# Two transformer layers on one core: the second layer's steps joined to the first's

## The chip, the cores and the metric

One core of one Trainium2 chip runs the whole kernel. Its engines work side by side, each in its own order: TensorE (PE in the profile) for matmuls, with its weight loads (PEld); VectorE (DVE); ScalarE (ACT), which alone computes exponentials and the like; GpSimd (POOL), which can't read the matmul banks; and SyncE (SP), which issues most DMAs. Matmuls write into eight banks of 128 x 512 floats. The metric is the device time of one execution in microseconds, as the median of several runs.

## The reference

The input is `x` of 8 batches x 512 tokens x 256 features, in float32. Two layers follow. Each normalizes `x` by layernorm to `xn` and adds an attention and a feed-forward branch of the same `xn`:

```
x = x + attn0(xn) + experts(xn)          # layer 0
x = x + attn1(xn) + ffn1(xn)             # layer 1, xn of the new x
attn0:   16 heads of 16, softmax(q k^T) v
experts: each token goes to one of 8 experts (argmax), layernorm, 256 -> 1024 relu -> 256, gated
attn1:   causal attention with q, k, v -> ctx; convolution over 3 tokens of ctx -> q2;
         causal attention with q2 and the same k, v; output projection
ffn1:    x U1 (rank 64) V1 + b1 -> gelu (tanh form) -> U2 (rank 64) V2 + b2
```

## The kernel before

**Jobs and steps.** Attention is cut into jobs of four heads of one batch: 32 in layer 0, 64 in layer 1 (32 with q, "firsts", and 32 with q2, "seconds", which come seven jobs later). A job of layer 0 has 8 steps and one of layer 1 has 6 (`STEPS`). In one step `run` issues matmuls for the row maxima of one job (`scores`, L345, reduced on DVE at L362 or L365) and, interleaved with them on other 32-row strips of the array, the scores for the exponentials of the job 12 steps behind (`exps`, L394, exponentials on ACT at L421, in layer 1 with a small mask matmul, L412). Between the two a job's maxima are transposed and DMAed into spare rows of q (`shift`, L375 to L382). `attend` (L434) multiplies by the values at the places that `AV_AT` gives.

**The order of the rest.** All five engines run in the order in which the code issues (`manual_schedule`). Other work is cut into pieces in a `Work` list, each with an earliest step, a deadline and a cost; `fill` issues some at the end of each step, ahead of that step's `attend`. In layer 0 a `stream` is paced beside it at `MOE_PER_STEP` of cost a step: first norms, routing, then 23 expert blocks (L772 features, L794 hidden, L815 output) and then the second norms (`SECOND`), one entry a step: gathers of the experts' rows by POOL (`g`), their weighted sum into `acc` on DVE (`+` and `P`, L522), statistics on DVE (`s`, `S`), the closing of a group with a square root on ACT (`c`, L247), normalizing on ACT (`n`, `N`, L257) and transposes to features (`f`, L266).

**The seam.** Layer 0's `run` comes to its end before anything else starts. Then comes a stage for the FFN alone: per batch one `ffn_in` (L965), four pairs of `ffn_hidden` (L977, gelu by ACT at L983) and `ffn_rank` (L990, summed up in bank 7), and `ffn_out` (L1002, L1006), with the second norms of batches 4 to 7 (`THIRD`) between. Only then does `run` start on layer 1 with a list of its own, `todo1`. Its pieces are q and k projections (`l1_project`, L293, 512 columns), values (L303), convolution (`convolve`, L1072, in halves of 256 columns, taken up on DVE), `to_tokens` (L1090), `to_features` (L266) and `project_out` (L1124).

**Banks in layer 1.** `banks_alone` gives three banks to the maxima, three to the scores, one to AV and one, bank 7, to all pieces.

Of the kernel before, what the change touches and what calls it, by code (L numbers as in the profile page):

```python
# [9 lines left out]
F32 = mybir.dt.float32  # L10
# [10 lines left out]
NB = 8  # L21
# [17 lines left out]
LEAD = (12, 12)  # L39
EARLY = 4  # L40
MOE_PER_STEP = 2.08
LAG = 7

# [17 lines left out]

SECOND = (
    "g0 g1", "", "", "+0", "P0 g2", "+1", "P1 g3", "", "+2", "P2 g4", "+3", "P3 g5", "s0", "S0 s1", "S1 s2", "S2 s3",
    "S3", "c", "n0", "N0 n1", "f0 N1", "n2 f1", "N2", "n3 f2", "N3", "f3",
)

THIRD = (
    "+4", "P4 s4 g6", "S4 +5", "P5 s5 g7", "S5 +6", "P6 s6", "S6 +7", "P7 s7", "S7", "c", "n4", "N4 f4", "", "n5",
    "N5 f5", "", "n6", "N6 f6", "", "n7", "N7 f7",
)  # L70

# [14 lines left out]
    {2: (0,), 4: (1,), 6: (2,), 8: (3,)}, {5: (0,), 6: (1, 3), 7: (2,)}, {2: (0,), 4: (1, 3), 6: (2,)},  # L86
# [10 lines left out]
class Work:  # L97
# [20 lines left out]
    def fill(self, t, per_step, most):  # L118
# [3 lines left out]
        while True:  # L122
# [19 lines left out]
            n += 1  # L142
# [10 lines left out]
def block_kernel(ctx: ExitStack, tc: tile.TileContext, x, a0_wqk, a0_bqk, a0_wv, a0_bv, cent, experts,  # L153
# [40 lines left out]
    for _ in range(2):  # L194
        value_buffer(const)
    banks = [psum.tile([P, S], F32, name=f"bank{i}") for i in range(8)]
# [14 lines left out]
    def banks_alone():  # L211
        share_banks(mx=banks[:3], sc=banks[3:6], av=banks[6:7], mm=banks[7:])

# [75 lines left out]
    def project(w, col, src, nm):  # L289

        ps = bank()
        for k in range(2):
            nc.tensor.matmul(  # L293
                ps, lhsT=w[:, k, col : col + P], rhs=src[:, k, :], start=(k == 0), stop=(k == 1)
            )
        return ps

    def values(w, bias, src, dst, h, nm):
        ps = bank()
        for j in range(2):  # L300
            c = 2 * h + j
            for k in range(2):
                nc.tensor.matmul(  # L303
                    ps[:, j * D : (j + 1) * D],
                    lhsT=src[:, k, c * P : (c + 1) * P],
                    rhs=w[:, k, :],
                    start=(k == 0),
                    stop=(k == 1),
                )
        for j in range(2):  # L310
            nc.vector.tensor_tensor(
                dst[:, 2 * h + j, :, 0:HD],
# [6 lines left out]
    class Job:  # L319


        def __init__(self, nm, causal, scale, v, g, done, pool):
            self.nm, self.causal, self.scale, self.v, self.g, self.done = nm, causal, scale, v, g, done
            self.pool = pool
# [7 lines left out]
        def scores(self, i):  # L332
# [24 lines left out]
            def after():  # L357
                for h in (2 * pr, 2 * pr + 1):
                    for qc, at, nk in parts:
                        src = heads[h % 2][:, at : at + nk]  # L360
                        if not self.causal:
                            nc.vector.tensor_reduce(self.m[:, qc, h, :], src, AX.X, ALU.max, negate=True)  # L362
                            continue
                        junk = l1.tile([P, S], BF16, tag="junk", name=f"jk{self.nm}_{qc}_{h}", bufs=1)
                        nc.vector.tensor_tensor_reduce(  # L365
                            out=junk[:, :nk], in0=src, in1=cmask[:, S - nk :], scale=1.0, scalar=-3e38,
# [17 lines left out]
        def exps(self, i):  # L384
# [22 lines left out]
            def after():  # L407
                if self.causal:
# [7 lines left out]
                e = self.pool.tile(  # L416
                    [P, 2, n], F32, tag=f"e{blocks[0]}" if self.causal else "e", name=f"e{self.nm}_{i}",
                    bufs=3 if self.causal else 4,
                )
# [22 lines left out]
    def run(jobs, work_of, layer, per_step, most):  # L442
        steps, lead = STEPS[layer], LEAD[layer]
        end = steps * len(jobs)
        if layer == 1:
            for job in jobs[-(lead // steps) :]:
                job.seq = 2
        attends = {}
        for j, job in enumerate(jobs):
            av_at = AV_AT[job.seq]  # L450
            for i, blocks in av_at.items():
                attends.setdefault(lead + steps * j + i, []).append((job, blocks, i == max(av_at)))

        def attend(t):
            for job, blocks, last in attends.pop(t, ()):
                for kc in blocks:
                    job.attend(kc, kc == 0, last and kc == blocks[-1])
                if last:
                    job.done(job, t)

        work_of.first()
        for t in range(max(attends) + 1):
            work_of.t = t
            if layer == 0 and t == lead:
                banks_alone()
            mm, after = [], []
            if t >= lead or layer == 1:
                maxima = (t,)
            else:

                maxima = (t, t + 1) if t % 2 == 0 else ()

            scores = (t - lead,) if t < end else (t - lead, t - lead + 1) if (t - end) % 2 == 0 else ()
            if t == end:
                banks_last()
            for at, call in [(i, Job.scores) for i in maxima] + [(i, Job.exps) for i in scores]:
                j, i = divmod(at, steps)
                if 0 <= j < len(jobs):
                    m, a = call(jobs[j], i)
                    mm.append(m)  # L480
                    after.append(a)
# [6 lines left out]
            work_of.fill(t, per_step, most)  # L488
            attend(t)
        work_of.drain()  # L490

    fgs, yns, norms_of = {}, {}, {}

    def second(pieces):

        for p in pieces.split():
            do, b = p[0], int(p[1:] or 0)
            if do == "c":
                norms_of[max(norms_of)].close()
                continue  # L500
            if do == "s":
                first = b < EARLY
                bs = range(EARLY) if first else range(EARLY, NB)
                if bs[0] not in norms_of:
                    norms_of[bs[0]] = Norms(mid, bs, "dc"[first], False)
            n = norms_of.get(0 if b < EARLY else EARLY)
            if do == "g":

                fgs[b] = mid.tile([P, NC, D], F32, tag="fg", name=f"fg{b}", bufs=2)
                for c in range(NC):  # L510
                    t = b * NC + c
                    nc.gpsimd.indirect_dma_start(
                        out=fgs[b][:, c, :],
# [4 lines left out]
            elif do in "+P":  # L518
                for c in range(2) if do == "+" else range(2, NC):
                    t = b * NC + c  # L520
                    a = acc[b][:, c, :]
                    nc.vector.scalar_tensor_tensor(  # L522
                        a, fgs[b][:, c, :], alpha[:, t : t + 1], a, ALU.mult, ALU.add
                    )
            elif do in "sS":
                n.stats(n.bs.index(b), range(2) if do == "s" else range(2, NC))
            elif do in "nN":
                if do == "n":
                    yns[b] = work.tile([P, NC, D], F32, tag="o", name=f"yn{b}")
                n.norm(n.bs.index(b), yns[b], range(2) if do == "n" else range(2, NC))  # L530
            else:
                t = big.tile([P, 2, S], F32, tag="xT", name=f"yT{b}")
                for k in range(2):
                    to_features(yns[b], t, 0, k, f"c{b}")
                xT1.append(t)
# [9 lines left out]
    mids = ExitStack()  # L545
    mid = mids.enter_context(tc.tile_pool(name="mid", bufs=1, side="right"))

    u1_sb = mid.tile([P, 2, 2, RANK], F32, name="u1_sb")
    v1_sb = mid.tile([P, FF], F32, name="v1_sb")
    v2_sb = mid.tile([P, D], F32, name="v2_sb")  # L550
    fb1_sb = mid.tile([P, NFC], F32, name="fb1_sb")
    u2_sb = mid.tile([P, NFC, RANK], F32, name="u2_sb")
    ob_sb = const.tile([P, D], F32, name="ob_sb")

    def load_ffn():
        for i in range(2):
            r = slice(i * RANK, (i + 1) * RANK)
            nc.sync.dma_start(out=u1_sb[:, :, i, :], in_=u1)
            nc.sync.dma_start(out=v1_sb[r, :], in_=v1)
            nc.sync.dma_start(out=v2_sb[r, :], in_=v2)  # L560
        nc.sync.dma_start(out=fb1_sb, in_=f_b1)
# [706 lines left out]
```

## Time and profile before

| | us |
|---|---|
| three runs | 2121.31, 2112.47, 2118.51 |
| median | 2118.51 |
| the profiled execution, its own time | 2120.86 |
| the profiled execution, first to last instruction | 2118.7 |

| stretch (us) | what runs |
|---|---|
| 0 to 951 | layer 0 with norms, routing and experts; the last expert output ends near 949 |
| 951 to 1020 | the rest of layer 0's attention, second norms of batches 0 to 3 |
| 1020 to 1133 | the FFN stage, second norms of batches 4 to 7 |
| 1133 to 1186 | layer 1's first 17 steps, without AV |
| 1186 to 2119 | layer 1 |

The profile's lines show one execution. "L345" is line 345 of the kernel before. A float32 matmul shows as two instructions (passes), a transpose as one. Their ends are modelled, so the distance from start to start tells more than the duration. The granted clock is the share of TensorE's full speed that the throttle allowed.

### The profile page before, as it was taken

How to read it: one execution, taken by the hardware profiler on the slowest of the kernel's cores; microseconds unless marked ns; L12 is line 12 of the kernel's file. 1: busy time of each engine (PE TensorE's matmuls, PEld its weight loads, DVE VectorE, ACT ScalarE, POOL GpSimd, SP SyncE). 2: the span in 40 equal slices, each digit the busy share in tenths (PEclk: the TensorE clock that was granted, in tenths of full speed). 3: DMA queues.
4: the chain of work that ended last, by engine and by line, in shares of the span. 5: the costliest groups of instructions: out<-in, count | busy, mean ns of one | idle time of the engine just before them, and what ended most of it. 6: DMA issues, size and time to landing. Idle time of an engine off the chain costs nothing.

```text
span 2118.7 us, 35530 instructions
## 1 busy us (share of the span) xinstructions
PE 2010.6 (95%) x13672; PEld 1016.4 (48%) x13672; DVE 1228.6 (58%) x3565; ACT 867.8 (41%) x1690; POOL 175.6 (8%) x222
## 2 busy tenths in 40 slices
PE   5797999999999999998898999999999999999998
PEld 3333555555555555552233445455555545554554
DVE  5564455555555555557424676666766666666763
ACT  4342333333333333335551444444444444444434
POOL 4153000000000000004211000000000000000000
PEclk8698999999999999999999899999999999999999
DMA  6014212212121221202100000000000000000000
GB/s 211 13 45 143 104 54 105 101 58 105 53 105 53 105 105 53 105 11 78 40 1 1 2 2 2 2 2 12 2 12 2 12 2 12 2 11 2 2 12 21
DMA packets 37192, 93.53 MB, mean 44 GB/s; under 512 B 5920, under 2 KB 28064, under 8 KB 34080
## 3 DMA queue, kind: packets, MB, share of 16 engines
q0 software_dynamic: 6384, 59.78, 7.7%
q1 hardware_dynamic: 29792, 30.56, 4.5%
q8 instruction: 107, 1.75, 0.3%
q10 hardware_dynamic: 848, 0.93, 0.1%
q14 instruction: 61, 0.50, 0.1%
HBM read 70.03 MB, written 20.45 MB: 43 GB/s over the span
## 4 chain that ended last, share of the span: by engine, by line
PE 83%; DVE 6%; issue 5%; DMA 4%; ACT 2%; POOL 1%; ACTq 0%; POOLq 0%; DVEq 0%; SPq 0%
PE bank L345 27%; PE bank L434 12%; PE bank L794 8%; PE bank L815 8%; PE bank L293 5%; PE bank L1072 4%; PE bank L412 4%; DMA hs_d<-h,pos_i 4%; PE bank L394 3%; PE bank L303 2%; PE bank L1090 2%; PE bank L1124 1%; DVE m L362 1%; PE bank L977 1%; PE bank L990 1%
## 5 line engine op out<-in xcount | busy, mean ns | idle before, releaser
L421 ACT ACTIVATE e<-bank 128x512 f32<-128x512 f32 (+1 forms) x1280 | 638.9, 552 | 921.4 <-PE bank L394 462.8
L345 PE MATMUL bank<-k,q 32*128 32x512 f32 (+3 forms) x3072 | 765.1, 538 | 24.6 <-DVE m L362 20.3
L394 PE MATMUL bank<-q,k 32*128 32x512 f32 (+3 forms) x3072 | 682.6, 535 | 2.4 <-DVE m L362 1.6
L365 DVE CUSTOM_DVE_ANT_0 jk<-bank,cmask 128x512 bf16<-128x512 f32 (+3 forms) x1024 | 502.8, 491 | 241.7 <-PE bank L345 162.4
L345 PEld LDWEIGHTS bank<-k,q 32*128 32x128 f32 x3072 | 301.4, 187 | 388.4 <-issue 165.2
L362 DVE TENSOR_REDUCE m<-bank 128x1 f32<-128x512 f32 x512 | 328.8, 685 | 152.5 <-PE bank L394 122.7
L434 PE MATMUL bank<-e,v 128*32 128x512 f32 (+3 forms) x3072 | 317.8, 501 | 0.7 <-ACT e L421 0.7
L394 PEld LDWEIGHTS bank<-q,k 32*128 32x128 f32 x3072 | 266.0, 186 | 12.2 <-issue 6.1
L794 PE MATMUL bank<-hsT,w 128*128 128x256 f32 x736 | 181.2, 392 | 6.4 <-DVE hsT L777 6.4
L794 PEld LDWEIGHTS bank<-hsT,w 128*128 128x128 f32 x736 | 135.1, 192 | 74.5 <-issue 58.9
L815 PE MATMUL bank<-w,hT 128*128 128x256 f32 x736 | 170.7, 385 | 0.0
L815 PEld LDWEIGHTS bank<-w,hT 128*128 128x128 f32 x736 | 137.5, 192 | 36.6 <-issue 18.7
L434 PEld LDWEIGHTS bank<-e,v 128*32 128x32 f32 x3072 | 67.7, 108 | 139.7 <-issue 133.0
L412 PE MATMUL bank<-mask_t,ident_bf 128*128 128x128 bf16 (+1 forms) x768 | 123.4, 244 | 0.0
L412 PEld LDWEIGHTS <-ident_bf 128*128 128x128 bf16 x768 | 43.9, 97 | 155.7 <-issue 140.6
L807 DVE TENSOR_SCALAR hT<-bank,w 128x256 f32<-128x256 f32 x92 | 44.5, 484 | 113.7 <-ACT hT L805 113.7
L1072 PE MATMUL bank<-ctxT,cw_sb 128*128 128x256 f32 x384 | 90.0, 383 | 2.1 <-DVE q L283 1.8
L365 DVE DVE_READ_ACCUMULATOR2_ANT m<- 128x1 f32 x1024 | 85.0, 83 | 0.0
L805 ACT ACTIVATE hT<-bank,w 128x256 f32<-128x256 f32 x92 | 43.7, 475 | 92.9 <-PE bank L794 92.9
L824 DVE TENSOR_TENSOR f<-bank,w 128x256 f32<-128x256 f32 x46 | 19.5, 425 | 105.4 <-PE bank L815 105.4
L285 ACT ACTIVATE k<-bank,bqk,rows 128x512 f32<-128x512 f32 x64 | 46.3, 774 | 81.7 <-PE bank L293 72.4
L1072 PEld LDWEIGHTS bank<-ctxT,cw_sb 128*128 128x128 f32 x384 | 70.1, 189 | 13.2 <-DVE q L283 3.2
(186 smaller groups left out, 1383.5 us busy)
## 6 DMA issues: line engine op xcount, KB each, us to landing
q<-mT SPq DMA_DIRECT2D x384, 2.0 KB
hs_d<-zeros SPq DMA_DIRECT2D x23, 256.0 KB
hs<-hs_d SPq DMA_DIRECT2D x23, 256.0 KB
fs_d<-f SPq DMA_DIRECT2D x23, 256.0 KB
acc<-in_x SPq DMA_DIRECT2D x8, 512.0 KB
out<-acc SPq DMA_DIRECT2D x8, 512.0 KB
cw_sb<-in_conv_w SPq DMA_DIRECT2D x1, 768.0 KB
wqk<-in_a_wqk ACTq DMA_DIRECT2D x1, 512.0 KB
```

The lines of the kernel that those rows point to most:

```text
L285: nc.scalar.activation(dst, ps, AF.Identity, bias=bias[:, half : half + 1], scale=rows[:, half : half + 1])
L293: nc.tensor.matmul(ps, lhsT=w[:, k, col : col + P], rhs=src[:, k, :], start=(k == 0), stop=(k == 1))
L345: lambda h=h, qc=qc, at=at, nk=nk: nc.tensor.matmul(heads[h % 2][:, at : at + nk], lhsT=self.q[h * PH : (h + 1) * PH, qc * P : (qc + 1) * ...
L362: nc.vector.tensor_reduce(self.m[:, qc, h, :], src, AX.X, ALU.max, negate=True)
L365: nc.vector.tensor_tensor_reduce(out=junk[:, :nk], in0=src, in1=cmask[:, S - nk :], scale=1.0, scalar=-3e38, op0=ALU.add, op1=ALU.max, acc ...
L394: lambda h=h, kc=kc, at=at, lo=lo: nc.tensor.matmul(heads[h % 2][:, at : at + S - lo], lhsT=self.k[h * PH : (h + 1) * PH, kc * P : (kc + 1 ...
L412: nc.tensor.matmul(heads[h][:, : len(blocks) * P], lhsT=ident_bf, rhs=mask_t[:, : len(blocks) * P], start=False, stop=True,)
L421: nc.scalar.activation(e[:, h, :], heads[h][:, :n], AF.Exp, scale=self.scale)
L434: nc.tensor.matmul(self.av[h * PH : (h + 1) * PH, lo:], lhsT=self.v[:, kc, 4 * self.g + h, :], rhs=es[h // 2][:, h % 2, :], start=first, s ...
L794: nc.tensor.matmul(ps[:, i * TB : (i + 1) * TB], lhsT=w[:, O_W1 + k * FF + fc * P : O_W1 + k * FF + (fc + 1) * P], rhs=self.hsT[:, k, :], ...
L815: nc.tensor.matmul(ps[:, 0:D], lhsT=self.hT[:, fc, j * P : (j + 1) * P], rhs=w[:, O_W2 + fc * D : O_W2 + (fc + 1) * D], start=(fc == 0), s ...
L1072: nc.tensor.matmul(ps[:, :w], lhsT=cw_sb[:, k, tap, c * P : (c + 1) * P], rhs=ctxT[b % 2][:, k, tap + lo : tap + lo + w], start=(k == 0 an ...
```

## The change

- **One run.** `run` takes the jobs of both layers. Layer 1's first job has its step 0 at step 256 (`T0`), right after layer 0's last maxima, so its maxima run beside layer 0's last 12 steps of exponentials. The separate FFN stage is gone. All pieces are in one list, `todo`.
- **Opening layer 1.** When the expert stream ends (step 240 in the order of instructions), the gathers of batch 0 are issued, layer 1's buffers are made and cleared, and all its weights are loaded by SP (`open_layer1`). `SECOND`, `THIRD` and three further entries for each of batches 5 to 7 are put at fixed steps; norms are closed in four groups instead of two.
- **Sums on GpSimd.** The gathered rows' weighted sum is two GpSimd instructions a chunk instead of one on DVE. There is one gather buffer instead of two.
- **FFN units.** A unit (`ffn_unit`) is two hidden chunks at place 3 of a job; the place of a step t is `(t - TS) % 6`, with `TS` = 268, layer 1's first step of exponentials. The gelu is made of Identity and Square on ACT, an add and a product on GpSimd, Tanh on ACT and a product on DVE, in the steps after; `rank` comes five steps later and sums on DVE.
- **Halved pieces in four of six steps.** `fill_evenly` spreads the pieces' costs over places 1 to 4 of a job; places 5 and 0 have AV. Projections have 256 columns (64 pieces for 32), the convolution 128 (64 for 32), values and output projection one chunk of tokens. In places 1 to 4 the pieces have bank 6 as well as bank 7 (`banks_between`).
- **AV in two bursts:** kc 0 at place 5, then 1, 3 and 2 at place 0 of the next.
- The convolution's results are taken up by ACT instead of DVE. The causal mask is bf16. Tiles are used in turn from fixed rings (`take_turn`) where pools gave them out.

The core of the diff:

```diff
-MOE_PER_STEP = 2.08
+MOE_PER_STEP = 2.07
+NORM_GROUPS = ((0,), (1,), (2, 3), (4, 5, 6, 7))
 SECOND = (
-    "g0 g1", "", "", "+0", "P0 g2", "+1", "P1 g3", "", "+2", "P2 g4", "+3", "P3 g5", "s0", "S0 s1", "S1 s2", "S2 s3",
-    "S3", "c", "n0", "N0 n1", "f0 N1", "n2 f1", "N2", "n3 f2", "N3", "f3",
+    "g0", "+0", "", "s0", "S0", "c0 n0", "N0", "f0", "g1", "+1", "", "", "s1", "", "S1", "c1 n1", "N1", "f1", "g2", "+2",
+    "", "", "s2", "", "S2", "g3", "+3", "", "", "s3", "", "S3", "c2 n2", "N2", "f2",
 )
 AV_AT = (
-    {2: (0,), 4: (1,), 6: (2,), 8: (3,)}, {5: (0,), 6: (1, 3), 7: (2,)}, {2: (0,), 4: (1, 3), 6: (2,)},
+    {2: (0,), 4: (1,), 6: (2,), 8: (3,)}, {5: (0,), 6: (1, 3, 2)}, {2: (0,), 4: (1, 3), 6: (2,)},
 )
...
+    def banks_between(free):
+        share_banks(mm=banks[6:] if free else banks[7:])
...
+        def free(t):
+            return t < TS or 0 < (t - TS) % STEPS[1] < 5
...
+            if t >= end:
+                todo.fill(t, 99.0, 1)
+            elif "pool" in l1:
+                if t >= TS + STEPS[1]:
+                    banks_between(free(t))
+                todo.fill_evenly(t, free)
+            else:
+                todo.fill(t, MOE_PER_STEP, 99)
...
-                    nc.vector.scalar_tensor_tensor(
-                        a, fgs[b][:, c, :], alpha[:, t : t + 1], a, ALU.mult, ALU.add
-                    )
+                    nc.gpsimd.tensor_scalar(fg[:, c, :], fg[:, c, :], alpha[:, t : t + 1], None, ALU.mult)
+                    nc.gpsimd.tensor_tensor(a, a, fg[:, c, :], ALU.add)
...
+            later.close()
+            l0.close()
+            second(SECOND[0])
+            open_layer1()
+            t = todo.t
+            at = [(t + i, p) for i, p in enumerate(SECOND)][1:]
+            at += [(t + len(SECOND) + THIRD_EVERY * i, p) for i, p in enumerate(THIRD)]
+            at += [(jobs1_at(b) - LATE + 2 * i, f"{p}{b}") for b in range(5, NB) for i, p in enumerate("nNf")]
...
+    def ffn_unit(b, c2):
+        hid, cub = wide(7), wide(3)
+        ps = [bank() for _ in range(2)]
+        for i in range(2):
+            fc, r = 2 * c2 + i, slice(i * RANK, (i + 1) * RANK)
+            nc.tensor.matmul(
+                ps[i], lhsT=l1["v1"][r, fc * P : (fc + 1) * P], rhs=l1["pT"][r, :], start=True, stop=True
+            )
+        for i in range(2):
+            fc = 2 * c2 + i
+            nc.scalar.activation(
+                hid[:, i * S : (i + 1) * S], ps[i], AF.Identity, bias=l1["fb1"][:, fc : fc + 1]
+            )
+        nc.scalar.activation(cub, hid, AF.Square, scale=GELU_C ** 0.5)
+        def times(i):
+            nc.vector.scalar_tensor_tensor(c, c, 1.0, u, ALU.add, ALU.mult)
+        def cube(i):
+            nc.gpsimd.tensor_scalar(c, c, 1.0, None, ALU.add)
+            nc.gpsimd.tensor_tensor(c, c, u, ALU.mult)
+        def tanh(i):
+            nc.scalar.activation(c, c, AF.Tanh, scale=GELU_A)
...
+        for after, f, i in ((1, cube, 0), (1, cube, 1), (2, tanh, 0), (3, tanh, 1), (3, times, 0), (4, times, 1)):
+            todo.add(t + after, t + after, 0.0, lambda f=f, i=i: f(i))
+        todo.add(t + 5, t + 5, 0.9, rank)
...
-    def convolve(n, half):
+    def convolve(n, quarter):
...
-            take(ps[:, :w], i, cb_sb[:, c, :], job.q[:, lo : lo + w], "v")
+            take(ps, i, l1["cb"][:, c, :], job.q[:, lo : lo + P], "s")
...
+    def ffn_at(n):
+        return TS + STEPS[1] * (1 + n * 17 // 10) + 3
```

## The prediction

> **What bounds the kernel now.** I read the page's busy line first, then the stages in stretches of 50 us, then TensorE's order of time in one job of layer 1 and across the seam between the layers.
>
> ```profile
> PE 2010.6 (95%) x13672; PEld 1016.4 (48%) x13672; DVE 1228.6 (58%) x3565; ACT 867.8 (41%) x1690; POOL 175.6 (8%) x222
> ```
> ```profile
> 900.00:950.00 50.00, 50.00 (x275) 27.33 (x273) 26.58 (x49) 16.97 (x32) 1.46 (x2) 1.00 0.02 6
> 950.00:1000.00 50.00, 45.07 (x241) 14.02 (x234) 37.71 (x92) 26.66 (x48) 25.89 (x26) 0.93 0.30 88
> ...
> 1050.00:1100.00 50.00, 45.52 (x177) 17.31 (x176) 13.39 (x25) 29.15 (x49) 9.42 (x4) 1.00 0.00 1
> ...
> 1150.00:1200.00 50.00, 48.14 (x234) 22.04 (x232) 28.11 (x107) 13.70 (x26) 0.00 (x0) 0.69 0.01 1
> ...
> 1500.00:1550.00 50.00, 49.60 (x430) 27.56 (x429) 34.01 (x123) 22.29 (x46) 0.00 (x0) 1.00 0.02 8
> ```
> The columns are PE, weight loads, DVE, ACT, POOL (us and count), then granted clock. Layer 0 with the experts (900) and layer 1 (1500) are full of TensorE work. The poor stretch is the seam. At 950 the experts have ended, DVE (37.7 of 50) paces the last scores. The FFN stage runs TensorE alone with DVE idle. At 1150 layer 1 starts with half-filled steps at a clock of 0.69.
>
> ```profile
> 984.66 0.59 PE L345 MATMUL bank<-k,q 32*128 32x512 f32 x1
> ...
> 1028.30 1.13 PE L977 MATMUL bank<-pT,v_sb 64*128 64x512 f32 x4
> 1029.36 1.08 PE L990 MATMUL bank<-gT,u_sb 128*64 128x512 f32 x4
> 1030.36 1.13 PE L977 MATMUL bank<-pT,v_sb 64*128 64x512 f32 x4
> ...
> 1185.63 1.94 PE L434 MATMUL bank<-e,v 128*32 128x512 f32 x8
> ...
> 1506.65 0.28 PE L345 MATMUL bank<-k,q 32*128 32x128 f32 x2
> ...
> 1506.76 0.28 PE L345 MATMUL bank<-k,q 32*128 32x128 f32 x2
> ...
> 1506.98 0.39 PE L412 MATMUL bank<-mask_t,ident_bf 128*128 128x256 bf16 x2
> 1507.30 1.20 PE L345 MATMUL bank<-k,q 32*128 32x256 f32 x3
> ```
> Starts matter here, since ends are modelled. Layer 0's last score is at 984.7, layer 1's first AV at 1185.6. A gelu unit costs TensorE 1.06 + 1.00 us. So **the FFN stage (1020 to 1133) is itself nearly all TensorE work**; moving it into layer 1 does not hide it. What can be won is the seam's emptiness.
>
> **The change, by three stretches.** The sum is made on the profiled execution: span 2118.7, its own time 2120.9, the median of three 2118.5; a difference is carried over as it is.
>
> *To 951 us (last expert output):* same pieces. The expert stream ends one step later (step 240, not 239, by the order of instructions) with the same work before it. Rings of tiles for pools, the bf16 mask, and the FFN loads moved: zero, as TensorE covers them.
>
> *The seam, 951 to the first AV of layer 1, today 234 us,* becomes steps 241 to 272. Sixteen steps still carry layer 0's scores; such steps took 949.3 to 984.7 today, 2.2 us each: 36. Eleven steps pair layer 1's maxima with layer 0's exponentials: 1.07 for four 512-wide tiles, 0.5 for AV, about 0.9 for a piece: 27. Five more are plain layer 1: 11. That is 74. On top come waits. POOL issues the first gathers until about 957.5 (4 x 1.25 from 952.8), clears the new buffers (the 1.81 memset row and smaller ones, 3), then does the first sums, four times 0.553 + 0.726: 966. The statistics are put on DVE three steps after the gather, about 958, and everything behind them on DVE, the maxima above all, waits: 5 to 8. SP also issues 2.95 MB of loads in that step (by their shapes; 0.36 to 0.43 each to issue, 6 us); the next query-row DMAs behind them come eight steps later and are safe, but the gathers share the engines: 0 to 8. Each closing of norms puts two table loads (1.283 each) on ACT with exponentials queued behind: about 3, three times. The statistics of the three further batches may wait likewise, 0 to 5 each. I take 6 + 2 + 9 + 2 = 19; from both sides 6 to 41. **Seam 93, so 141 saved** (119 to 154).
>
> *Layer 1, 1185.6 to the end, today 933 us.* Prices are TensorE start to start.
>
> ```profile
> L1072 PE MATMUL bank<-ctxT,cw_sb 128*128 128x256 f32 x384 | 90.0, 383 | 2.1 <-DVE q L283 1.8
> L1072 PEld LDWEIGHTS bank<-ctxT,cw_sb 128*128 128x128 f32 x384 | 70.1, 189 | 13.2 <-DVE q L283 3.2 <-ACT ctxT L270 1.3
> L983 ACT ACTIVATE gT<-bank,fb_sb 128x512 f32<-128x512 f32 x64 | 40.4, 684 | 49.0 <-PE bank L977 49.0
> L899 POOL TENSOR_TENSOR acc<-acc,og 128x256 f32<-128x256 f32 x32 | 23.2, 726 | 603.7 <-DVE og L895 603.6
> L1148 POOL TENSOR_TENSOR acc<-acc,ob_sb 128x1024 f32<-128x1024 f32 x8 | 18.8, 2351 | 74.7 <-DVE acc L1006 74.7
> ```
> - FFN arrives: 32 x (1.06 + 1.00), seven entry projections at 1.92, eight outputs at 1.92: **+95**. Features of batches 2 to 7, 48 transposes at 0.147: **+7**.
> - Halved projections: a pass of 256 columns streams in 0.213 and a burst adds about 0.15. 54 halves at 1.0 against 28 wholes at 1.87: +2. Values and output projection cut likewise: +3.
> - Convolution in quarters: 64 pieces of 12 passes of 128 columns replace 32 of 12 passes of 256, which took 3.0 each, 96 in all. The weight loads double. A load's record lasts 0.189, more than the 0.107 that 128 columns need, so the price lies between 64 x (12 x 0.107 + 0.15) = 92 and 64 x (12 x 0.189 + 0.15) = 155. The lines at 1506.65 and 1506.76 are nearest: two passes of 128 columns, each with its own 128-column load of 0.19, start 0.11 apart, so loads overlap. But those are 32-row tiles. I take 0.12: 102, **+6** (-4 to +59).
> - AV in two bursts: 1.00 + 1.00 + 0.57 holds about 0.15 a burst beyond streaming; 64 fewer: **-10**.
> - The wait at 1507.30 (the second head starts 0.7 late, DVE still reducing) comes once in most jobs. Longer, filled steps cover it: **-25** (0 to -42).
> - New waits. A unit puts two Identity (0.68 each by the gelu row) and a Square (about 1.0) on ACT; the next exponentials queue behind these 2.4 us, and with three score banks a short next step waits. Each cube half on POOL is 2 x 0.553 + half of 2.35 = 2.3. Counted from the start of the unit's step, its matmuls end at +2.3, ACT's three at +4.8, the cubes at +7.2 and +9.5; with steps of 2.5, 2.9, 1.8 and 2.7 us the tanhs reach the head of ACT at +6.8 and +9.5. The fit is tight: each microsecond that POOL is late blocks ACT, the exponentials and the AV copy behind it. In steps 278 and 314 the cubes stand behind a batch's sums (5.1 on POOL). The last closing adds 3. **+30** (0 to +64).
>
> Other engines keep room. DVE (34 of 50) gains about 47 for the products, 22 for the rank sums, 41 for features, statistics and outputs, and loses 32 as ACT takes over the convolution: some 70% of the new stretch. ACT gains about 165 (56%).
>
> Sum: 95 + 7 + 5 + 6 - 10 - 25 + 30 = +108, so 1041. **Total 951 + 93 + 1041 = 2085 span, 33 less; 2085 on the median too.**
>
> **Two rules of the Trainium skill.** "TensorE: Matmul & The Clock Gate", Back-to-back issue gap, speaks against quarters: pairs of load and matmul sustain about 81 ns at 128 columns where streaming alone takes 56. Scaled so, a pass would be 0.155 and the sum 27 higher, about 2112; the trace's 0.11 on row tiles disagrees. "ScalarE: Activation LUTs", Table sets, puts exp and tanh in one set, sqrt in another, at about 2.7 us a load; the trace's loads last 1.283, and by the page's figure four closings would cost some 11 more.
>
> **The rivals.**
> 1. *Slower: quarters are bound by weight loads.* For it: 0.189 is longer than 0.107. Against: the overlapped row-tile loads. At 0.189 the convolution costs 53 more than I took: 2138. It turns the result slower than 2129 from about 0.177 a pass.
> 2. *No change: the cube chain blocks ACT.* For it: the fit to a few tenths; ACT is in order and exponentials are the feed of AV. One extra microsecond in each of 32 units: 2117. Against: units stand 6 or 12 steps apart.
> 3. *The seam does not close.* If the chain gather, sums, statistics, norm, features, projection is late for both first batches, TensorE drains and the clock falls as at 1150: 40 more, 2125. Against: 15 steps lie between the gather and the first layer 1 score.
> 4. *More is won:* all hidden DVE waits go (17 more) and the new waits stay at 10 (20 less): 2048.
>
> **How the numbers follow.** A measurement here tells about 0.5% from no change, so faster is below 2108, slower above 2129. Forecast 0.50 (2060 to 2108), rival 4 0.12, rivals 2 and 3 0.21 (mostly 2108 to 2129, a third of it beyond), rival 1 or several together 0.17. Faster 0.62, same 0.14, slower 0.24. The convolution (+53), the waits (+34) and the seam (+22) do not all fall at once; the range 2040 to 2145 leaves about 0.18 outside.
>
> **What would show it.** Right: no stretch without layer-1 or layer-0 scores, first layer-1 AV near 1044, no low clock after 951, jobs of about 16.5 us where they take 14.5 now, convolution passes starting 0.11 to 0.13 apart. Wrong: passes near 0.19; ACT idle before tanh with POOL as releaser and TensorE waiting for exponentials; DVE idle before the first statistics by more than 8 us; a cold clock near 960.

## The result, and the profile after

The changed kernel takes 2146.7 us (median of four runs, 2142.2 to 2150.6) where the kernel before took 2117.8 beside it: the ratio is 1.0138, with a 95% interval of 1.0106 to 1.0170. It is slower by 29 us; the prediction was 33 us faster. The profiled execution has a span of 2147.5.

The page's busy line and the same 50 us stretches (PE, weight loads, DVE, ACT, POOL, granted clock, DMA):

```profile
PE 1984.3 (92%) x14168; PEld 1027.1 (48%) x14168; DVE 1252.2 (58%) x3611; ACT 995.2 (46%) x1950; POOL 403.1 (19%) x414
```
```profile
900.00:950.00 50.00, 49.24 (x268) 26.07 (x266) 25.44 (x47) 16.25 (x30) 1.45 (x2) 1.00 0.02 6
950.00:1000.00 50.00, 42.12 (x208) 14.13 (x204) 27.56 (x58) 23.04 (x42) 27.54 (x35) 0.86 0.34 88
1000.00:1050.00 50.00, 44.96 (x233) 18.97 (x233) 30.03 (x111) 23.63 (x44) 24.63 (x27) 0.90 0.08 22
1050.00:1100.00 50.00, 44.53 (x316) 21.65 (x315) 32.09 (x118) 27.71 (x53) 20.71 (x19) 0.90 0.05 12
...
1500.00:1550.00 50.00, 46.23 (x404) 24.46 (x404) 32.85 (x118) 26.19 (x54) 7.84 (x5) 1.00 0.04 12
```

TensorE's busy time fell by 26 us, yet the span grew by 29. In the middle of layer 1 (1500) TensorE now stands at 46.2 of 50, where it was 49.6; no other engine is near full. Something makes TensorE wait. The view of TensorE's waits over layer 1 (line, what it waited for, total us, times, longest) names it; first the kernel before, then the seven longest of the changed kernel's 39 rows:

```profile
PE bank L1090 <- DVE q L283: 4.0, 14, 0.3
PE bank L1090 <- ACT avs L1106: 2.6, 2, 2.0
PE bank L1072 <- DVE q L283: 1.8, 8, 0.2
PE bank L266 <- DVE o L1094: 0.4, 1, 0.4
```
```profile
PE bank L1124 <- DVE mT L429: 11.2, 12, 1.7
PE bank L356 <- DVE mT L429: 7.0, 6, 1.3
PE bank L426 <- ACT avs L1158: 7.0, 12, 1.9
PE bank L1142 <- DVE mT L429: 4.3, 8, 0.9
PE bank L320 <- ACT xT L1052: 3.9, 5, 0.8
PE bank L1142 <- ACT avs L1158: 3.5, 3, 1.9
PE bank L1174 <- DVE mT L429: 3.2, 3, 1.3
```

The first list is all there was: 9 us. The seven rows of the second hold 40 of 75 us. There, quarters of the convolution (L1124), values (L356), AV transposes (L1142) and output projections (L1174) wait for `mT`: the copy out of the bank that `shift` had filled (31 us in all rows). One such wait in the changed kernel's timeline, on TensorE, DVE and ACT (start, length, [idle before, and who ended it]):

```profile
1352.46 0.58 ACT L1158 COPY avs<-bank 128x512 f32<-128x512 f32 x1
...
1353.60 0.27 PE L426 MATMUL bank<-ident,m 128*16 128x128 f32 x1
...
1353.71 0.60 PE L1142 MATMUL bank<-ident,avs 128*128 128x128 f32 x4
1353.79 0.56 DVE L416 CUSTOM_DVE_ANT_0 junk<-bank,cmask 128x384 bf16<-128x384 f32 x1
...
1355.19 0.56 DVE L416 CUSTOM_DVE_ANT_0 junk<-bank,cmask 128x384 bf16<-128x384 f32 x1
...
1355.67 0.27 DVE L429 TENSOR_SCALAR mT<-bank 16x128 f32<-16x128 f32 x1
1356.00 1.60 PE L1124 MATMUL bank<-ctxT,cw 128*128 128x128 f32 x12 [1.69 <-DVE mT L429]
```

In a job's second step `shift`'s small transpose takes one of the two piece banks (in 12 of the 64 jobs it waits for ACT's copy of AV, as that bank held AV), and the AV transposes take the other. The third piece wants the first bank again. Its copy needs 0.27 us, but it stands on DVE behind the maxima of the whole step and ends two microseconds after the transpose. The kernel before packed one piece a step, so nobody stood behind.

I summed TensorE's order by starts, from the first AV of layer 1 to TensorE's last instruction, and took out the idle time that the trace marks. The work is 915 us before (from 1185.6) and 1004 after (from 1060.3); the marked waits are 8.8 before and **75.3** after. This count of work and waits is used below. A stall that the trace does not mark counts as work in it.

### The profile page after: what moved, and what is told of

Its sections match the earlier page's. It is cut to its first block, busy times and chain, and to the rows that moved or that the text cites. A ratio compares the mean times of both kernels' runs of the same rounds, so it can differ in the third digit from the quotient of the medians.

```text
span 2147.5 us, 36982 instructions
## 1 busy us (share of the span) xinstructions
PE 1984.3 (92%) x14168; PEld 1027.1 (48%) x14168; DVE 1252.2 (58%) x3611; ACT 995.2 (46%) x1950; POOL 403.1 (19%) x414
## 5 line engine op out<-in xcount | busy, mean ns | idle before, releaser
L469 ACT ACTIVATE e<-bank 128x512 f32<-128x512 f32 (+1 forms) x1280 | 639.4, 552 | 830.6 <-PE bank L445 480.5
L397 PE MATMUL bank<-k,q 32*128 32x512 f32 (+1 forms) x3056 | 724.5, 536 | 25.5 <-DVE m L414 23.6
L416 DVE CUSTOM_DVE_ANT_0 junk<-bank,cmask 128x512 bf16<-128x512 f32 (+3 forms) x1024 | 502.5, 491 | 352.3 <-PE bank L397 277.2
L397 PEld LDWEIGHTS bank<-k,q 32*128 32x128 f32 x3056 | 267.7, 186 | 410.2 <-issue 160.1
L445 PEld LDWEIGHTS bank<-q,k 32*128 32x128 f32 x3072 | 250.0, 185 | 16.5 <-ACT e L469 9.6
L1065 POOL TENSOR_SCALAR xT<-xT 128x512 f32<-128x512 f32 x64 | 95.3, 1489 | 605.5 <-ACT xT L1057 524.7
L347 PE MATMUL bank<-xT,wqk 128*128 128x256 f32 (+1 forms) x384 | 134.2, 479 | 11.9 <-DVE q L337 4.8
L938 POOL TENSOR_TENSOR acc<-acc,og 128x256 f32<-128x256 f32 x32 | 23.2, 725 | 591.2 <-DVE og L934 591.1
L463 PE MATMUL bank<-mask_t,ident_bf 128*128 128x128 bf16 (+1 forms) x768 | 122.9, 243 | 0.0
L463 PEld LDWEIGHTS <-ident_bf 128*128 128x128 bf16 x768 | 43.9, 97 | 155.0 <-issue 139.7
L1124 PE MATMUL bank<-ctxT,cw 128*128 128x128 f32 x768 | 100.4, 281 | 13.1 <-DVE mT L429 11.2
L1124 PEld LDWEIGHTS bank<-ctxT,cw 128*128 128x128 f32 x768 | 92.0, 194 | 23.3 <-DVE mT L429 14.3
L347 PEld LDWEIGHTS bank<-xT,wqk 128*128 128x128 f32 x384 | 68.8, 196 | 70.1 <-issue 42.2
```

The costliest lines, as they stand in the source:

```text
L347: nc.tensor.matmul(ps, lhsT=w[:, k, col : col + P], rhs=src[:, k, tokens], start=(k == 0), stop=(k == 1))
L397: lambda h=h, qc=qc, at=at, nk=nk: nc.tensor.matmul(heads[h % 2][:, at : at + nk], lhsT=self.q[h * PH : (h + 1) * PH, qc * P : (qc + 1) * ...
L416: nc.vector.tensor_tensor_reduce(out=l1["junk"][:, :nk], in0=src, in1=l1["cmask"][:, S - nk :], scale=1.0, scalar=-3e38, op0=ALU.add, op1= ...
L445: lambda h=h, kc=kc, at=at, lo=lo: nc.tensor.matmul(heads[h % 2][:, at : at + S - lo], lhsT=self.k[h * PH : (h + 1) * PH, kc * P : (kc + 1 ...
L463: nc.tensor.matmul(heads[h][:, : len(blocks) * P], lhsT=ident_bf, rhs=mask_t[:, : len(blocks) * P], start=False, stop=True,)
L469: nc.scalar.activation(e[:, h, :], heads[h][:, :n], AF.Exp, scale=self.scale)
```

## The experiments

All were measured beside the kernel before, on one chip per group. The kernel before took 2120 to 2125 in these groups and 2118 beside the changed kernel, so where two runs of different groups are compared, a range is given: by the medians, by the ratios and by the spans of the profiled executions.

**The order of the two banks.** After, each step starts the ring afresh, so `shift` always takes the bank that AV has just held.

```
     def banks_between(free):
-        share_banks(mm=banks[6:] if free else banks[7:])
+        if len(rings["mm"]) != 1 + free:
+            share_banks(mm=[banks[7], banks[6]] if free else banks[7:])
```

> The changed kernel with one edit: the ring of the two piece banks is no longer reset in every step, and begins with bank 7 at place 1. As it stands, the first piece of each step always takes bank 6: at place 1 that is the shift, which must wait until ACT has copied AV out of it (TensorE waited 7.0 us for that in all), and a step's first piece meets the one before it in the same bank. Theory (banks): that 7.0 and some of the 10 us of waits for q, k and Identity go, 8 to 18 us less than the changed kernel's 2147, so about 2134; the waits behind the shift's copy on DVE stay near 30. Rival (the tanh chain or the convolution's quarters are what costs): no more than 3 us less.

Measured: 2139.4 us, ratio 1.0079 (1.0055 to 1.0103). `shift`'s wait for ACT's copy (7.0 us) is gone, and now the AV transposes wait 6.6 for it; the waits for `mT` stay at 29. Some 7 to 12 us of the loss are the order.

**Shift ahead of the maxima.** On top of the bank order, `shift` is issued ahead of that step's maxima on DVE, not behind them.

```
+            if t in shift_at:
+                banks_between(free(t))
+                shift_at.pop(t)()
             for f in after:
                 f()
...
-        todo.add(t0 + STEPS[1], t0 + STEPS[1] + 1, 0.2, job.shift)
+        at = t0 + STEPS[1] + 1
+        if TS + STEPS[1] <= at < T0 + STEPS[1] * (2 * NB * HG):
+            shift_at[at] = job.shift
+        else:
+            todo.add(at - 1, at, 0.2, job.shift)
```

> The edit of the run before, and the shift at place 1 is issued before that step's maxima are put on DVE, not after them, so that its copy out of the bank (0.27 us) is not queued behind 2.0 us of maxima. In the changed kernel TensorE waits 31 us in all for that copy, with a later piece of the same step wanting the bank. Theory (banks): these 31 us go nearly whole, with e1 about 2105 to 2115. Rival (the tanh chain, which blocks ACT, is behind it): the waits turn into waits for ACT in the same steps, and no more than 10 us are won over e1.

Measured: 2119.3 us, ratio 0.9995 (0.9967 to 1.0023), 20 less than with the order alone; the waits for `mT` are zero. The forecast of 2105 to 2115 was missed by four: waits on the next copies took part of it. In this kernel's waits (its line numbers are one to five higher) the AV transposes and the pieces behind them are on top:

```profile
PE bank L1147 <- ACT avs L1163: 8.1, 13, 1.9
PE bank L483 <- ACT k L340: 5.3, 5, 1.4
PE bank L1080 <- DVE o L1151: 4.5, 9, 1.0
```

**AV transposes one step later**, on top of both.

```
-        todo.add(t + 1, t + 2, 0.5, lambda: to_tokens(job, av_sb))
+        todo.add(t + 2, t + 2, 0.5, lambda: to_tokens(job, av_sb))
...
-                todo.add(t + 2 + k, t + 2 + k, 0.5, lambda k=k: to_features(o, l1["ctxT"][b % 2], 1, k, f"d{b}"))
+                todo.add(t + 3 + k, t + 3 + k, 0.5, lambda k=k: to_features(o, l1["ctxT"][b % 2], 1, k, f"d{b}"))
...
-            todo.add(t + 2 + k, t + 5, 0.5, lambda k=k: to_features(o, cT, 0, k, f"e{b}"))
+            todo.add(t + 3 + k, t + 5, 0.5, lambda k=k: to_features(o, cT, 0, k, f"e{b}"))
```

> The version with the bank order kept and the shift ahead of the maxima (2119), and the four transposes of a job's AV one step later (only in the step t + 2; the feature transposes behind them one step later too). In that version's trace the transposes wait 11 us for ACT's copy of AV, and pieces behind them 10 us for DVE's o. Theory: the first goes wholly and some of the second: 2104 to 2112. Rival: these waits only cover others (a score's wait for DVE comes next): 2115 to 2121.

Measured: 2097.1 us, ratio 0.9883 (0.9858 to 0.9908): faster than both kernels, by more than its waits lost (57 to 43), since work on TensorE also packs closer (998 to 985). Layer 1 now takes 1039 us of its span of 2094.3.

**The same edit alone**, on the changed kernel with its bank order and `shift` as they were.

> The changed kernel (2147) with the AV transposes one step later and nothing else. If the wait for ACT's copy of AV is a cost of its own, the gain is that of the other pair (2119 to 2097): 2123 to 2129. If the shift's copy behind the maxima on DVE holds the banks in the same steps and ends last, little of it shows: 2138 to 2146.

Measured: 2110.0 us, ratio 0.9946 (0.9918 to 0.9973). Neither expectation held: this edit alone brings 39 us of span (2147.5 to 2108.4; 37 by the medians, 41 by the ratios), more than the other two together. Of the 39, four lie ahead of the first AV of layer 1. Behind it the marked waits fall from 75 to 52 and the work by 12. The waits for `mT` fall from 31 to 12 without a change to `shift`. The timeline shows how:

```profile
1340.34 0.27 PE L426 MATMUL bank<-ident,m 128*16 128x128 f32 x1
...
1340.45 1.50 PE L1124 MATMUL bank<-ctxT,cw 128*128 128x128 f32 x12
...
1342.06 0.27 DVE L429 TENSOR_SCALAR mT<-bank 16x128 f32<-16x128 f32 x1
```

`mT`'s copy still starts 1.7 us after its transpose, but the quarter finds the other bank free and starts 0.11 after `shift`. The AV transposes come a step later, when their copy has long ended: their wait for it falls from 3.5 to 0.7, while `shift`'s stays (7.0 to 6.4). So the cost lies in three takers of two banks meeting in one step; the next run tests this from the other side.

**Shift one step later instead.** The other of the two is moved out of the meeting.

```
-        todo.add(t0 + STEPS[1], t0 + STEPS[1] + 1, 0.2, job.shift)
+        todo.add(t0 + STEPS[1] + 2, t0 + STEPS[1] + 2, 0.2, job.shift)
```

> The changed kernel with the shift's transpose in the step after the one in which it is now, AV transposes left where they are. If the meeting of the two in one step over two banks is the cost, most of the 38 that moving the AV transposes brought comes here too: 2112 to 2128. If the AV transposes' own wait for ACT's copy is the cost, it stays: 2138 to 2150.

Measured: 2130.6 us, ratio 1.0063 (1.0032 to 1.0094). It is 16 us shorter than the changed kernel (20 by the spans), about half of what the AV transposes brought, and just outside what was expected. The waits for `mT` fall to 7, but `shift` now waits where it stands:

```profile
PE bank L426 <- DVE o L1146: 18.2, 25, 1.4
PE bank L426 <- DVE q L337: 5.2, 7, 1.2
```

So the meeting is confirmed in kind; which of them should leave it depends on whose copy is late.

**The same edit in the kernel before.**

> The kernel before with the same edit to its AV transposes (one step later, the feature transposes behind them too). It packs one piece a step, and its trace shows 2.6 us of waits for ACT's copy of AV and 0.4 for o. Theory (the wait is one that the change made by packing several pieces into a step): 2115 to 2125, no change. Rival (the edit is worth as much in the kernel before, whatever the change did): 2080 to 2100.

Measured: 2134.0 us, ratio 1.0078 (1.0051 to 1.0105): there the edit costs 14, where no change was expected. The rival (it would help any of the two) fell: the wait that it cures is one that the change made. In the kernel before, the second feature transposes of a batch then wait 10.5 us for the first ones' copy out of the one bank, which stands on DVE behind maxima.

**AV in the older of the two banks**, on top of the 2097 version.

```
+        old = rings["mm"]
+        if free and len(old) == 1:
+            share_banks(mm=old + rings["av"])
+        elif not free and len(old) == 2:
+            share_banks(av=old[:1], mm=old[1:])
...
-        share_banks(sc=banks[:5], av=banks[6:7], mm=banks[5:6] + banks[7:])
+        share_banks(sc=banks[:5], mm=banks[5:6] + rings["mm"][:1])
```

> The version with the bank order kept, the shift ahead of the maxima and the AV transposes one step later (2097), and AV takes whichever of the two piece banks was used longer ago instead of always the same one. In that version's trace AV waits 8.7 us for a piece's bias copy (k and q, on ACT and DVE) out of its bank. Theory: that goes, and 0 to 5 more with it: 2083 to 2091. Rival: the other bank's copy ends as late, so nothing is won: 2094 to 2100.

Measured: 2099.5 us, ratio 0.9899 (0.9868 to 0.9931); the rival held. AV's waits fell from 8.7 to 0.9, and the same time came back in the scores and the gelu pieces.

**No cubes on GpSimd.**

```
-        for after, f, i in ((1, cube, 0), (1, cube, 1), (2, tanh, 0), (3, tanh, 1), (3, times, 0), (4, times, 1)):
+        for after, f, i in ((2, tanh, 0), (3, tanh, 1), (3, times, 0), (4, times, 1)):
```

> The changed kernel without the two GpSimd operations of each gelu half (the add of 1 and the product with u; the tanh is taken of the square alone), so 64 x (1.49 + 1.27) = 177 us of GpSimd work and the wait of each tanh for it are gone; the result is not the reference's. My theory (pieces wait for banks whose copies stand behind the maxima on DVE) gives at most 8 us less than the changed kernel's 2147. The rival (the chain cube to tanh holds ACT and the exponentials behind it) gives 25 us less or more: 2122 or below.

Measured: 2140.2 us, ratio 1.0085 (1.0057 to 1.0114), some 7 to 11 less. The waits for `mT` are no fewer (37 us), those for ACT's copy of AV fall from 10.5 to 6.4. My second rival, the chain from cube to tanh, costs about this much; it is not what ate most of the gain.

**Gelu from ACT's table.**

```
-                hid[:, i * S : (i + 1) * S], ps[i], AF.Identity, bias=l1["fb1"][:, fc : fc + 1]
+                cub[:, i * S : (i + 1) * S], ps[i], AF.Gelu_apprx_tanh, bias=l1["fb1"][:, fc : fc + 1]
...
-        nc.scalar.activation(cub, hid, AF.Square, scale=GELU_C ** 0.5)
...
-        for after, f, i in ((1, cube, 0), (1, cube, 1), (2, tanh, 0), (3, tanh, 1), (3, times, 0), (4, times, 1)):
-            todo.add(t + after, t + after, 0.0, lambda f=f, i=i: f(i))
-        todo.add(t + 5, t + 5, 0.9, rank)
+        todo.add(t + 2, t + 2, 0.9, rank)
```

> The changed kernel with gelu taken from ACT's table in one instruction per half, as the kernel before had it (no Identity, Square, tanh, cube or product; the second product of a unit follows two steps behind the first instead of five). ACT loses 5 passes of a unit and gets 2 of 0.68 and up to two table loads of 1.28. My theory: exponentials come up to 2.6 later after a unit, DVE has 64 products fewer, and the bank waits stay: 2152, from 2137 to 2172. If the tanh-made unit's own waits were what ate the gain, it is 2120 or below; if the table loads block the exponentials with nothing to hide them, 32 x 2.6 = 83 more: 2200 or above.

Measured: 2191.4 us, ratio 1.0326 (1.0287 to 1.0364): 40 to 45 more than the changed kernel, where I expected 5, and short of the 83 for loads with no cover. Besides the lines shown, the sum's factor of 0.5 went and the FFN's outputs come three steps sooner. The groups on ACT in layer 1 show 66 table loads, two a unit, and its waits show pieces that want a bank back from the gelu halves (L1052), first behind such a load:

```profile
L469 ACT ACT_TABLE_LOAD x34 | 43.6, 1283 | 11.9 <-PE bank L463 11.5
L1052 ACT ACT_TABLE_LOAD x32 | 41.1, 1283 | 1.0
```
```profile
PE bank L320 <- ACT xT L1052: 11.0, 7, 2.1
PE bank L347 <- ACT xT L1052: 10.2, 10, 2.1
PE bank L1119 <- ACT xT L1052: 10.2, 13, 2.1
```

The marked waits are 21 us more than in the changed kernel (35 of them for these halves, where it has 7), and the scores take 22 longer. So inside layer 1 the tanh-made unit is the better one. That the table loads are the reason is likely, but the edit moves the second product as well, and no run separates the two.

**The convolution in halves**, as before the change.

```
-        lo = quarter * P
+        lo, w = quarter * S // 2, S // 2
...
-                for quarter in range(4):
+                for quarter in range(2):
```

> One part of the change undone: the convolution in 32 pieces of 256 columns instead of 64 of 128. In the changed kernel a quarter takes 1.53 us start to start, 12 passes at 0.115 and 0.15 for the burst, so it is not bound by weight loads at 0.19. Theory: 64 x 1.53 = 98 becomes 32 x 2.75 = 88, 10 less, and fewer pieces meet in a step, but each holds its bank longer: 2130 to 2145. Rival (the quarters' weight loads cost what I feared): 40 or more less, below 2107.

Measured: 2160.4 us, ratio 1.0180 (1.0140 to 1.0220), 9 to 14 more than the changed kernel, where 2 to 17 less was expected; the two intervals overlap a little. The convolution's own time falls from 95 to 88, but the scores, which the longer pieces now stand ahead of, take 18 longer. The rival that saw weight loads behind the quarters fell, and halves win nothing in this packing.

**Pieces over all six steps**, on the version with `shift` ahead of the maxima.

```
-                todo.fill_evenly(t, free)
+                todo.fill_evenly(t, lambda u: True)
```

> The version with the bank order kept and the shift ahead of the maxima (2119), and the pieces spread over all six steps of a job instead of four. If the cost of the change lies in several pieces sharing two banks in one step, fewer meet there: 2100 to 2112. Rival: in the fifth and the first step AV holds the second bank, so pieces put there wait for one another's copy, and PE waits for the single bank: 2125 to 2145.

Measured: 2146.4 us, ratio 1.0116 (1.0089 to 1.0143), 26 to 27 more than its base. That is the rival's size (1 us above its range), but not its cause: the marked waits are even 7 us fewer, and it is the scores' own stretch that grows, by some 30. Why it does was not settled. Four steps of six is the better choice here.

**Second norms' sums on DVE.**

```
-      nc.gpsimd.tensor_scalar(fg[:, c, :], fg[:, c, :], alpha[:, t : t + 1], None, ALU.mult)
-      nc.gpsimd.tensor_tensor(a, a, fg[:, c, :], ALU.add)
+      nc.vector.scalar_tensor_tensor(a, fg[:, c, :], alpha[:, t : t + 1], a, ALU.mult, ALU.add)
```

> One part of the change undone: the gathered rows are weighted and summed by DVE again, one instruction a chunk just ahead of its statistics, instead of by two on GpSimd. In the changed kernel the first AV of layer 1 comes at 1060, 16 us later than forecast, and the granted clock falls to 0.7 to 0.9 in the stretches where DVE waits for GpSimd's sums. Theory (the statistics wait for GpSimd, TensorE drains, the clock falls): first AV 10 to 18 us earlier, the clock at 1.0 in most of the seam, 2128 to 2137 in all. Rival (the clock falls because the steps of the seam are thin, whoever sums): 5 us at most, and the clock stays low at the same places.

Measured: 2147.5 us, ratio 1.0126 (1.0088 to 1.0165), no difference that can be told from the changed kernel. I expected 10 to 18 less. TensorE's wait for the maxima near 965 shrank from 4.3 to 1.65, and the first AV came 4.4 sooner, as the rival allowed, but layer 1 was no shorter. The clock still fell to 0.83 and 0.66 in the two stretches of 10 us from 960, and then stood at 1.00 until 1050.

The same edit on the 2097 version:

> The version with the AV transposes later (2097), and the second norms' sums back on DVE, next to each batch's statistics. In the first such run (the changed kernel with this alone) the first AV of layer 1 came 4.4 us sooner and the rest took 0.9 longer. Theory: the same here, 3 to 5 less: 2092 to 2094. Rival: what DVE takes on in the seam and in the steps with statistics comes back as later copies: 2096 to 2104.

Measured: 2112.7 us, ratio 0.9948 (0.9921 to 0.9975), slower than its base, and by more than the rival allowed; the first AV comes 2.0 sooner and the rest takes some 10 longer. In this version the sums are better on GpSimd.

**All edits together:** bank order, shift ahead, AV transposes later, AV in the older bank, sums on DVE.

> All four edits and the sums on DVE together: bank order kept, shift ahead of the maxima, AV transposes later, AV in the older bank, sums on DVE. By the sum of the parts (2097, less 10, less 4): 2083, from 2074 to 2092, faster than the kernel before by 1.3 to 2.1%. Rival: the parts overlap and it stays where the transposes left it: 2095 to 2100.

Measured: 2105.9 us, ratio 0.9914 (0.9884 to 0.9944). Neither range was met, and the parts do not add up. The 2097 version keeps the lowest median, though its interval overlaps those of the version with AV in the older bank (2099.5) and of this run.

**A filled gap in the seam**, on the version with the AV transposes later alone.

```
+            if t == 245:
+                ps = bank()
+                for _ in range(9):
+                    nc.tensor.matmul(ps, lhsT=ident, rhs=turn["k"][-1], start=True, stop=True)
```

> The version with the AV transposes later alone (2110), and 9 matmuls of 512 columns (9 x 0.43 = 3.9 us) that nobody reads, put at the end of step 245, ahead of the 4.3 us in which TensorE waited for DVE. In that version the clock is 0.76, 0.67 and 0.89 in the three stretches of 10 us from 960. If the low clock comes from the gap and costs time: the clock stays above 0.95 and the first AV of layer 1 comes 3 to 6 us sooner than 1056.2, total 2104 to 2107. Rival: DVE sets the pace there in any case, so a full clock changes nothing, or the matmuls delay the chain: 2109 to 2115.

Measured: 2121.7 us, ratio 1.0015 (0.9992 to 1.0038), and it does not settle whether the clock costs time. The nine matmuls took 18 passes of 0.44, 8.0 us and not 3.9, so the first AV came 7.5 later. Of the gap of 4.3 us two short ones were left (0.85 and 1.36, at 971 and 973; the second is a wait for exponentials), and the clock fell all the same, a stretch later:

```profile
960.00:970.00 10.00, 10.00 (x42) 3.82 (x41) 6.07 (x16) 2.13 (x5) 6.98 (x9) 1.00 0.78 200
970.00:980.00 10.00, 7.00 (x28) 2.73 (x24) 3.52 (x7) 6.89 (x12) 3.38 (x2) 0.70 0.00 0
980.00:990.00 10.00, 8.76 (x48) 2.65 (x41) 4.32 (x8) 2.93 (x6) 8.99 (x11) 0.79 0.19 53
```

## Why the prediction was wrong, step by step

**To 951 us: right.** The last expert output starts at 945.4 and the next AV at 949.1.

**The seam: 93 forecast, 109 measured**, so 16 of the 62 us between forecast and result. I had taken 36 for the steps with layer 0's scores and 27 for those that pair both layers (fifteen and twelve by their numbers, where I wrote sixteen and eleven, a slip of 0.3 us), with 19 of waits beside them; they took about 52 and 45, waits included. The DVE stall that I priced at 5 to 8 is there, but smaller. DVE in the changed kernel's timeline:

```profile
962.01 0.43 DVE L293 BATCH_NORM_STATS2 stc<-acc 128x6 f32<-128x256 f32 x1 [2.23 <-POOL acc L576]
...
963.72 0.43 DVE L293 BATCH_NORM_STATS2 stc<-acc 128x6 f32<-128x256 f32 x1 [1.06 <-POOL acc L576]
```

DVE idles 3.3 us, TensorE 4.3. What I left out is the clock afterwards: 0.76, 0.67 and 0.88 in the three stretches of 10 us from 960, 0.81 and 0.68 in the two from 1000, 0.83 from 1050. Summing 10 x (1 - clock) gives some 14 us. It is a measure of size, not a proof: in the version with the AV transposes alone moved, the two stretches from 1000 stood at 1.00, and the first AV came 4.2 sooner with the same 4.3 gap ahead. Why the clock falls there was not settled. My third rival foresaw a falling clock and 40 more: the clock fell, and the seam grew by 16.

**Layer 1, the sums of work: right but for 10.** By the count of work, FFN is 103 (95 forecast), the masked diagonal matmuls (L463) 8 more (not forecast), the convolution +7.6 (+6), features +8 (+7), AV -9 (-10), scores -30 (-25 for the maxima stalls). Together with the smaller pieces the work grew by 89, and my terms without the new waits gave 78. That they come so close is in part errors that cancel: FFN and diagonal are 16 over, the scores and `shift`'s transposes (13 before, 8 now) 10 under. The 8 of the diagonal look like unmarked stalls rather than work: with the bank order alone kept, the same matmuls take 82 us, as they did before (83). The first rival, that quarters are bound by weight loads, fell: in the fence above, 12 passes start at 1340.45 and the next scores at 1341.88, 0.119 a pass, and I had taken 0.12 (in the changed kernel's fence, from 1356.00 to the next scores at 1357.53, it is 0.128). The estimate that the prediction scaled from the Trainium skill ("TensorE: Matmul & The Clock Gate", Back-to-back issue gap), 0.155 a pass, is not met by these passes.

**New waits, +30 (0 to +64): this step failed.** The marked waits grew by 66, and most of them have a cause that the sum does not name: pieces that wait for a bank, 31 us of them for `mT`'s copy alone. What I had priced was the gelu chain on ACT, and that part came true in its first half. ACT idles before the tanhs, with GpSimd as releaser, 31 us in all:

```profile
L1070 ACT ACTIVATE xT<-xT 128x512 f32<-128x512 f32 x64 | 40.5, 633 | 31.1 <-POOL xT L1066 31.1
```

That is 0.97 a unit. A cube half takes 2.76 us and not my 2.3, so a unit's two are 0.9 late. My second rival put 32 us on one extra microsecond a unit. But TensorE waits only 2.6 us for exponentials (L469) in all, and of its 10.5 for AV's copy some 4 follow such an idle ACT (at 1407.94, `shift` waits 0.37 for a copy behind a tanh that came 0.98 late). Without the cubes 7 to 11 us are won: the chain costs about that, and the 30 were put on the wrong queue.

The change gives two banks to pieces in four of six steps, and I priced no piece waiting for its bank; in the trace of before, with one piece a step, such waits come to 9 us. What I ought to have counted is, for each step, how many pieces take a bank, how many banks there are, and where on DVE or ACT each copy out stands. The rows were there. Before as well, `mT`'s copy started 1.4 us after the `shift` transpose that it follows:

```profile
1511.07 0.27 PE L375 MATMUL bank<-ident,m 128*16 128x128 f32 x1
...
1512.49 0.27 DVE L378 TENSOR_SCALAR mT<-bank 16x128 f32<-16x128 f32 x1
```

Of the prediction's signs of being wrong, the cold clock near 960 and ACT idle before tanh were seen. Passes near 0.19, TensorE waiting long for exponentials and DVE idle for more than 8 us were not.

The account: 16 for the seam, 36 for the waits and 10 for the work make 62, the distance from 2085 to 2147. The experiments say how firm its largest part is: moving the AV transposes, with the feature transposes behind them, by one step gives back 35 us of layer 1. With all three bank edits, layer 1 takes 1039 where 1041 was forecast, but that is partly luck, for 43 us of marked waits are left there and the forecast had 30 of another kind. The change's own idea is sound: with these edits it is 1.2% faster than the kernel before. The loss lies in a step's order that it took over from a packing of one piece.

## What to carry to other kernels

When a change packs more pieces into a step, count the takers of each buffer in that step, and for each the place of the copy that frees it in its engine's queue: here a copy of 0.27 us behind a step's other work held its bank for 2.3 us. Where a step is crowded, try the piece whose input comes latest one step later; the same move won 39 us in the crowded kernel and cost 14 in the one with one piece a step. Waits replace each other, so an edit's value depends on which others are made: here 7 to 12, then 20, then 22 to 24 in one order, and 37 to 41 for the last one alone.

## What was not expected of the hardware

On GpSimd, the `tensor_scalar` instructions with one operation took longer here than those with two. The groups on GpSimd in the changed kernel:

```profile
L1065 POOL TENSOR_SCALAR xT<-xT 128x512 f32<-128x512 f32 x64 | 95.3, 1489 | 605.5 <-ACT xT L1057 524.7
...
L575 POOL TENSOR_SCALAR xT<-xT,alpha 128x256 f32<-128x256 f32 x32 | 29.9, 934 | 0.3
...
L644 POOL TENSOR_SCALAR acc<-acc,rs1e,nme 128x256 f32<-128x256 f32 x16 | 8.8, 549 | 0.8
```

On 256 columns a multiply alone (L575) takes 934 ns, a multiply and an add (L644) 549. I had priced all by the second, so the cube halves took 2.76 us and not 2.3, and a batch's sums 1.68 a chunk and not 1.28. The operands differ too (L575 and L1065 work on other tiles than L644), and so does the work beside them (L644 runs before 183 us, L575 after 960), so the number of operations is the likely cause and not a shown one.
